# First and last batch of a four-layer graph attention kernel: other order of the first loads, norms by VectorE's statistics, and a last head in two halves

## The chip, the cores and the metric

The kernel runs on one core of one Trainium2 chip. The metric is the device time of one execution in microseconds, lower is better. The engines are named as in the profile: PE is TensorE's matmul (PEld its weight load), DVE is VectorE, ACT is ScalarE, POOL is GpSimd, SP is SyncE. `SPq` and `POOLq` are the queues from which transfers are issued. A line number such as L330 is a line of the kernel before.

## The reference

There are 16 graphs of 1024 nodes with 256 features, and a 0/1 adjacency matrix for each. Four graph attention layers follow one another; each normalizes its input, projects it, weights the neighbours, and adds the result to its input. The first and the last layer, cut to what matters:

```python
# x: (16, 1024, 256), adj: (16, 1024, 1024)
def _layernorm(x, axis=-1, eps=1e-5):
    m = jnp.mean(x, axis=axis, keepdims=True)
    v = jnp.var(x, axis=axis, keepdims=True)
    return (x - m) / jnp.sqrt(v + eps)

# layer 0 (layers 1 and 2 have other activations of the weight and an elu at the end)
h = jnp.maximum(_layernorm(x), 0.0)
Wh = jnp.einsum('bnf,fo->bno', h, W)
f1, f2 = Wh @ a1, Wh @ a2
e = jax.nn.leaky_relu(f1[:, :, None] + f2[:, None, :], negative_slope=0.2)
e = jnp.where(adj == 0, NEG_INF, e)
x = x + jnp.einsum('bij,bjo->bio', jax.nn.softmax(e, axis=-1), Wh)

# layer 3: the same with 4 heads of 64 features (only edges of type 1 occur), and then
out = jax.nn.relu(dst) + h            # dst: attention times values, plus bias
mu, var = out.mean(-1, keepdims=True), out.var(-1, keepdims=True)
out = (out - mu) / jnp.sqrt(var + 1e-6) * ln_gamma + ln_beta
x = x + out                           # heads side by side: 1024 x 256
```

## The kernel before, in words

All of the time below is in `short_path`; a general path stands behind a flag (`bad`) and isn't taken with these inputs. The nodes of a batch lie in eight blocks of 128 partitions; four pairs of blocks share a row of memory, so that a partition of a pair holds two neighbouring nodes (`in_blocks`).

**Two streams.** Even batches form stream 0 and odd batches stream 1. `batch(b)` is a generator that emits instructions and yields estimated times; the loop at the end of `short_path` always advances the stream that is behind, and stream 1 starts 111 (`LAG`) later. So the dependent stretches of one batch lie beside the matmuls of the other. Only at the very start is stream 0 alone, and only at the very end stream 1. The framework then orders each engine's instructions by priority and by a plan of its own; `keep_in_program_order` fixes the order of single instructions.

**Loading.** `load(b)` has POOL issue four transfers that cast a quarter of the adjacency matrix's rows each from int32 to bytes and write them to memory (`narrow`, L125), and then SP issue four transposing transfers (L135), one for each pair of blocks of columns, into `mask`. Each transpose reads all rows, so it waits for all four casts. `fetch_nodes` loads `x_b` with one transfer of 1 MB on SP (L115). The weights come in `prepare`, on SP too: for layers 0 to 2 first W and then the attention vectors `a`, copied to all partitions (L197); L225 multiplies the two and sums, and `extend` (L189) writes the products as extra columns of W.

**Layer 0's norm and projection.** `first(pair)` sums two blocks of x on DVE (L476); `project` scales the sums to `minus_mean` (L282), makes `centered`, max(x - mean, 0), on DVE (L285), and has ACT sum the squares (L292). `inverse_root` makes the reciprocal deviation on POOL with an add (L271) and a power (L272). PE transposes `centered` (L301), ACT copies it out as `hT` (L303), PE multiplies by the extended W (L308), and `evict` (L376 on ACT, L380 on DVE) makes the values V. In later layers the sums come from the end of the layer before.

**Attention.** PE lays the column of scores out as a row on all partitions (L337), DVE makes the weights for each block with one instruction (L330) from row, column and mask, and PE multiplies weights and V (L424).

**The last layer.** For each of four heads PE makes values and totals transposed (L541), ACT copies both out (L618), PE turns them (L625, L633), DVE inverts the totals (L627, L348, L349) and scales (L636) into `y`. Then `center(h)` adds the bias on POOL (L502), adds the projected input and takes the mean off on DVE (L503, L505 to L507), squares on ACT (L509) and sums on DVE (L511), with `inverse_root` on POOL. `rescale`, one head later, multiplies by the reciprocal deviation on DVE (L515), and by gamma and adds x on POOL (L516, L517). All of these work on 128 x 512 elements, a head of all eight blocks. At the end POOL issues two transfers of 512 KB to the output (L650). Squares of the adjacency (L154), which feed the flag, lie in between on ACT.

Of the kernel before, what the change touches and what calls it, by code (L numbers as in the profile page):

```python
# [41 lines left out]
P = 128  # L42
# [19 lines left out]
def short_path(ctx: ExitStack, tc: tile.TileContext, ins: dict, out: bass.AP, bad: bass.AP):  # L62
# [48 lines left out]
    narrows = [dram.tile([N, N // 2], BF, name=f"narrow{n}") for n in range(2)]  # L111

    def fetch_nodes(b: int):
        xs[b] = nodes.tile([P, NI, D], F32, name="x_b")
        fetch = nc.sync.dma_start(xs[b].rearrange("p (c t) f -> p c t f", t=2), in_blocks(x[b]))  # L115
        if b > 0:
            tc.keep_in_program_order(fetch)

    def load(b: int):
# [3 lines left out]
        rows = narrow.bitcast(U8).rearrange("(c t q) j -> c q t j", t=2, q=P)  # L123
        for c in range(NI // 2):
            cast = nc.gpsimd.dma_start(  # L125
                rows[c], adj[b, ts(c, 2 * P), :].rearrange("(q t) j -> q t j", t=2)
            )
            tc.keep_in_program_order(cast)
# [5 lines left out]
        for c in range(NI // 2):  # L134
            turn = nc.sync.dma_start_transpose(  # L135
                mask[:, c].rearrange("p n t -> p (n t)").bitcast(BF), narrow[:, ts(c, P)]
# [36 lines left out]
    def prepare():  # L173
# [21 lines left out]
        def fetch(l: int):  # L195
# [5 lines left out]
            if l < 3:  # L201
                begin(W[l][:, :, :D], ins[f"L{l}_W"].rearrange("(k p) o -> p k o", p=P))
                begin(scratch[l][:, : 2 * D], on_all_partitions(ins[f"L{l}_a"], 2 * D))
                return
# [63 lines left out]
    def inverse_root(squared: bass.AP, n: int, elements: int, eps: float) -> bass.AP:  # L268

        r = small.tile([P, n], F32, name=f"rstd{n}")  # L270
        nc.gpsimd.tensor_scalar_add(r, squared, elements * eps)  # L271
        nc.gpsimd.tensor_tensor(r, r, minus_half.to_broadcast([P, n]), op=ALU.pow)  # L272
        return r
# [4 lines left out]
    def project(b: int, l: int, xb: bass.AP, sums: bass.AP, pair: int, evict):  # L278


        minus_mean = small.tile([P, 2], F32, name="minus_mean")
        nc.vector.tensor_scalar_mul(minus_mean, sums[:, ts(pair, 2)], -1.0 / D)  # L282
        centered = work.tile([P, 2, D], F32, name="centered", bufs=3)
# [12 lines left out]
        rstd = inverse_root(squared, 2, D, LN_EPS)  # L296
# [67 lines left out]
    def batch(b: int):  # L364
# [110 lines left out]
        def first(pair: int):  # L475
            nc.vector.tensor_reduce(sums[:, ts(pair, 2)], xb[:, ts(pair, 2), :], AX.X, ALU.add)  # L476
# [19 lines left out]
        shape = [P, NI, E]  # L496

        def center(h: int):

            yh = y[:, :, h, :]  # L500
# [550 lines left out]
```

## Time and profile before

| what | value |
|---|---|
| median of 3 runs | 2948.88 us (2948.02 to 2951.19) |
| profiled execution, span | 2948.4 us |
| granted TensorE clock, mean | 0.992 |
| PE busy | 2810.6 us, 95% of the span |
| DVE busy | 2124.8 us, 72% |
| ACT busy, POOL busy | 1092.1 us (37%), 980.7 us (33%) |
| first attention weights (L330) start | 26.82 us |
| last attention weights (L330) end | 2908.45 us |
| second output transfer issued (L650) | about 2935.0 us |

PE's share is so high that what counts is where it is not busy. The page's picture in 40 slices shows that only the first slice and the last two fall below 0.9 of PE's time. Two instructions of one group can take different times, and a group's mean hides that, so the timeline is what tells when each step of the first and the last batch ran. The chain of waits names, for each step, what released it; pieces that follow one another on one engine are merged there.

### The profile page before, as it was taken

The page shows a single profiled execution, that of the slowest core. Times are in us where ns is not written, and L with a number is a line of the kernel's source. Part 1 is how long each engine was busy: PE and PEld are TensorE (multiplying, and loading weights), DVE is VectorE, ACT ScalarE, POOL GpSimd, SP SyncE. Part 2 cuts the span into 40 slices and gives each one's busy share as a digit, 9 for nine tenths or more (in the row PEclk, how much of TensorE's full clock was granted, in tenths as well). Part 3 has the DMA queues.
Part 4 walks back from the last instruction along what each step waited for, and adds up shares of the span by engine and source line. Part 5 has one row for each costly group of instructions (what it writes and reads, how often), then busy time and mean ns, then how long its engine had stood idle before and what let it go on. Part 6 is the DMA issues. An engine that isn't in the chain of part 4 may idle for free.

```text
span 2948.4 us, 44754 instructions
## 1 busy us (share of the span) xinstructions
PE 2810.6 (95%) x16790; PEld 1969.3 (67%) x16790; DVE 2124.8 (72%) x4471; ACT 1092.1 (37%) x3025; POOL 980.7 (33%) x1535
## 2 busy tenths in 40 slices
PE   7999999999999999999999999999999999999975
PEld 5775857668576685766758576685766857667551
DVE  5658688585976858678586875859768586785855
ACT  2333434343343433424333343433434334343331
POOL 2123324243233423324233242432334233242333
PEclk9999999999999999999999999999999999999997
DMA  7204022030311303122030220303113031010101
GB/s 123 40 8 65 29 31 56 8 51 29 42 45 19 68 1 51 36 29 58 8 52 29 33 55 8 51 29 45 43 20 67 1 51 36 15 30 8 22 18 27
DMA packets 120495, 106.11 MB, mean 36 GB/s; under 512 B 73680, under 2 KB 91216, under 8 KB 120272
## 3 DMA queue, kind: packets, MB, share of 16 engines
q0 software_dynamic: 40448, 67.12, 15.4%
q1 hardware_dynamic: 79824, 36.05, 5.5%
q8 instruction: 135, 2.21, 0.3%
q14 instruction: 88, 0.72, 0.1%
HBM read 153.49 MB, written 33.55 MB: 63 GB/s over the span
## 4 chain that ended last, share of the span: by engine, by line
PE 60%; DVE 23%; issue 8%; POOL 5%; ACT 3%; DMA 1%; POOLq 0%; SPq 0%; ACTq 0%; DVEq 0%
PE acc L424 36%; DVE weights L330 16%; PE acc L541 11%; PE acc L308 9%; PE misc L301 2%; POOL rstd L272 2%; POOL y L502 2%; ACT square L292 1%; DVE V L380 1%; PE row L337 1%; DVE y L503 1%; DVE var L511 1%; DVE y L507 1%; DVE mean L505 1%; ACT below L356 1%
## 5 line engine op out<-in xcount | busy, mean ns | idle before, releaser
L424 PE MATMUL acc<-V,weights 128*128 128x257 f32 x6144 | 1436.3, 385 | 33.9 <-DVE weights L330 16.7
L424 PEld LDWEIGHTS acc<-V,weights 128*128 128x128 f32 x6144 | 1141.9, 191 | 277.9 <-DVE weights L330 72.0
L541 PE MATMUL acc<-weights,V 128*32 128x512 f32 x6144 | 692.0, 597 | 12.1 <-DVE weights L330 8.1
L330 DVE SCALAR_TENSOR_TENSOR weights<-row,ex,mask 128x1024 f32<-128x1024 f32 x512 | 629.1, 1273 | 97.4 <-PE row L529 66.0
L308 PE MATMUL acc<-W,hT 128*128 128x259 f32 (+1 forms) x2048 | 516.5, 389 | 41.7 <-ACT hT L303 29.2
L330 DVE SCALAR_TENSOR_TENSOR weights<-row,V,mask 128x1024 f32<-128x1024 f32 x384 | 473.8, 1275 | 1.0 <-PE row L337 1.0
L308 PEld LDWEIGHTS acc<-W,hT 128*128 128x128 f32 x2048 | 379.6, 191 | 138.0 <-ACT hT L303 47.1
L541 PEld LDWEIGHTS acc<-weights,V 128*32 128x32 f32 x6144 | 189.6, 110 | 417.6 <-issue 410.7
L356 ACT ACTIVATE below<-acc,inv 128x256 f32<-128x256 f32 x256 | 121.1, 473 | 818.0 <-DVE inv L349 537.3
L272 POOL TENSOR_TENSOR rstd<-rstd,minus_half 128x2 f32<-128x2 f32 (+1 forms) x320 | 302.9, 947 | 20.3
L292 ACT ACTIVATE square<-x_b,minus_mean 128x256 bf16<-128x256 f32 x512 | 259.7, 507 | 111.1 <-DVE minus_mean L282 105.4
L404 POOL TENSOR_TENSOR x_b<-x_b,beta 128x256 f32<-128x256 f32 x128 | 93.4, 730 | 489.8 <-ACT square L292 489.8
L348 DVE TENSOR_SCALAR inv<-acc 128x1 f32<-128x1 f32 x256 | 39.2, 154 | 256.0 <-PE acc L424 254.7
L271 POOL TENSOR_SCALAR rstd<-squared 128x2 f32<-128x2 f32 x256 | 64.6, 253 | 462.8 <-ACT square L292 461.9
L303 ACT ACTIVATE hT<-misc 128x512 f32<-128x512 f32 x256 | 150.1, 592 | 119.7 <-PE misc L301 119.4
L359 DVE SCALAR_TENSOR_TENSOR x_b<-below,x_b 128x256 f32<-128x256 f32 x256 | 133.0, 519 | 85.3 <-ACT below L356 83.2
L618 ACT COPY sums<-acc 128x512 f32<-128x512 f32 x128 | 74.9, 585 | 307.8 <-PE acc L541 300.3
L285 DVE TENSOR_SCALAR centered<-x_b,minus_mean 128x256 f32<-128x256 f32 x512 | 182.6, 385 | 5.3
L376 ACT ACTIVATE V<-acc,rstd 128x3 f32<-128x3 f32 x384 | 98.4, 261 | 232.0 <-PE acc L308 231.3
L380 DVE TENSOR_SCALAR V<-acc,rstd,V 128x256 f32<-128x256 f32 x256 | 131.6, 537 | 62.0 <-ACT V L376 61.1
L301 PE MATMUL misc<-ident,centered 128*128 128x128 f32 x1024 | 157.9, 277 | 15.2 <-DVE centered L285 13.4
L149 POOL DMA_DIRECT2D adj_i<-in_adj_dram x128 | 74.7, 584 | 286.4 <-ACT adj_i L154 254.9
(88 smaller groups left out, 2210.0 us busy)
## 6 DMA issues: line engine op xcount, KB each, us to landing
adj_i<-in_adj_dram POOLq DMA_DIRECT2D x128, 256.0 KB, 3.9
x_b<-in_x_dram SPq DMA_DIRECT2D x16, 1024.0 KB, 6.4
narrow<-in_adj_dram POOLq DMA_DIRECT2D x64, 256.0 KB, 9.5
out_dram<-y POOLq DMA_DIRECT2D x32, 512.0 KB, 7.4
mask<-narrow SPq DMA_TRANSPOSE x64, 3.7
W<-in_L_gnn_W_dram SPq DMA_DIRECT2D x3, 256.0 KB, 5.8
weights<-in_L_gnn_a_dram SPq DMA_DIRECT2D x3, 256.0 KB, 8.1
W<-in_L_gnn_W_dram SPq DMA_DIRECT2D x2, 128.0 KB, 8.3
```

Source lines behind the costliest of these rows:

```text
L272: nc.gpsimd.tensor_tensor(r, r, minus_half.to_broadcast([P, n]), op=ALU.pow)
L285: nc.vector.tensor_scalar(centered[:, n, :], xb[:, 2 * pair + n, :], minus_mean[:, n : n + 1], 0.0, op0=ALU.add, op1=ALU.max,)
L292: nc.scalar.activation(square, xb[:, 2 * pair + n, :], AF.Square, bias=minus_mean[:, n : n + 1], accum_out=squared[:, n : n + 1],)
L301: nc.tensor.transpose(turned[:, k, ts(n, P)], centered[:, n, ts(k, P)], ident)
L303: nc.scalar.mul(hT, turned, ROOT_D)
L308: nc.tensor.matmul(projected, hT[:, k, ts(n, P)], W[l][:, k, :], start=(k == 0), stop=(k == NK - 1),)
L330: nc.vector.scalar_tensor_tensor(w, r, c(j), masks[b][:, j // 2, :, j % 2], op0=op, op1=ALU.mult)
L356: nc.scalar.activation(below, acc[:, :D], AF.Exp, scale=inv)
L359: nc.vector.scalar_tensor_tensor(xi, below, 1.0, xi, op0=ALU.min, op1=ALU.add)
L380: nc.vector.tensor_scalar(V[:, i, :D], projected[:, :D], rstd, V[:, i, D : D + 1], op0=ALU.mult, op1=ALU.mult,)
L424: nc.tensor.matmul(accs[i], weights[j][:, ts(i, P)], V[:, j, : D + 1], start=(j == 0), stop=(j == NI - 1),)
L541: made = nc.tensor.matmul(accT[ts(n, QUAD), :], values, moving, start=first, stop=last)
```

## The change

At the start, the loads of the first batch are meant to arrive in the order in which they are needed, and the norm of layer 0 in batch 0 to pass through fewer engines. `x` comes in four transfers on ACT's queue, one for each pair of blocks. The attention vectors are loaded before W. The casts of the first adjacency matrix are made by halves of its columns (`halves`), each half by two transfers, so that the first two transposes need only the first half. In batch 0 the mean and the variance come from DVE's bn_stats and bn_aggr in place of sums on DVE and squares on ACT.

At the end, in the last batch alone, the bias of the last two heads is added by DVE; the last head is centred and rescaled in two halves of four blocks; the last half's gamma and x steps go to DVE too; and the two outputs are issued by SP and ACT. `inverse_root` gets a factor for the variance and one buffer name for all larger sizes; `inv8` has three buffers for six.

```diff
 def fetch_nodes(b: int):
     xs[b] = nodes.tile([P, NI, D], F32, name="x_b")
+    if b == 0:
+        for c in range(NI // 2):
+            nc.scalar.dma_start(
+                xs[b][:, ts(c, 2), :],
+                x[b, ts(c, 2 * P), :].rearrange("(p t) f -> p t f", t=2),
+            )
+        return
...
+    if b == 0:
+        for h in range(NH):
+            for t in range(2):
+                cast = nc.gpsimd.dma_start(
+                    halves[h].bitcast(U8).rearrange("(c t q) j -> t c q j", t=2, q=P)[t],
+                    adj[b].rearrange("(c q t) j -> t c q j", t=2, q=P)[t, :, :, ts(h, HALF)],
+                )
+                tc.keep_in_program_order(cast)
...
-                mask[:, c].rearrange("p n t -> p (n t)").bitcast(BF), narrow[:, ts(c, P)]
+                mask[:, c].rearrange("p n t -> p (n t)").bitcast(BF),
+                halves[c // NH][:, ts(c % NH, P)] if b == 0 else narrow[:, ts(c, P)],
...
+                begin(scratch[l][:, : 2 * D], on_all_partitions(ins[f"L{l}_a"], 2 * D))
                 begin(W[l][:, :, :D], ins[f"L{l}_W"].rearrange("(k p) o -> p k o", p=P))
-                begin(scratch[l][:, : 2 * D], on_all_partitions(ins[f"L{l}_a"], 2 * D))
...
-        r = small.tile([P, n], F32, name=f"rstd{n}")
-        nc.gpsimd.tensor_scalar_add(r, squared, elements * eps)
+        r = small.tile([P, max(n, NI) if n > 2 else n], F32, name=f"rstd{8 if n > 2 else n}")[:, :n]
+        nc.gpsimd.tensor_scalar(r, squared, times, elements * eps, op0=ALU.mult, op1=ALU.add)
...
+        if sums is None:
+            mv = small.tile([P, 2, nc.vector.BN_AGGR_DIM], F32, name="mv", bufs=2)
+            for n in range(2):
+                stats = small.tile([P, nc.vector.BN_STATS_DIM], F32, name="stats", bufs=1)
+                nc.vector.bn_stats(stats, xb[:, 2 * pair + n, :])
+                nc.vector.bn_aggr(mv[:, n, :], stats)
+                nc.vector.tensor_scalar(
+                    centered[:, n, :], xb[:, 2 * pair + n, :], mv[:, n, 0:1], 0.0,
+                    op0=ALU.subtract, op1=ALU.max,
+                )
+            rstd = inverse_root(mv[:, :, 1], 2, D, LN_EPS, D)
...
+        def center(h: int, blocks=slice(0, NI), engine=nc.gpsimd):
+            yh = y[:, blocks, h, :]
...
-            nc.gpsimd.tensor_add(yh, yh, bias[:, head].unsqueeze(1).to_broadcast(shape))
+            engine.tensor_add(yh, yh, bias[:, head].unsqueeze(1).to_broadcast(shape))
...
+        def rescale(yh: bass.AP, blocks, head, rstd: bass.AP, engine=nc.gpsimd):
             nc.vector.tensor_mul(yh, yh, rstd.unsqueeze(2).to_broadcast(shape))
-            nc.gpsimd.tensor_mul(yh, yh, gamma[:, head].unsqueeze(1).to_broadcast(shape))
-            nc.gpsimd.tensor_add(yh, yh, xb[:, :, head])
+            engine.tensor_mul(yh, yh, gamma[:, head].unsqueeze(1).to_broadcast(shape))
+            engine.tensor_add(yh, yh, xb[:, blocks, head])
...
-            inv = small.tile([P, NH, NG], F32, name="inv8")
+            inv = small.tile([P, NH, NG], F32, name="inv8", bufs=3)
...
-            normed.append(center(h))
+            if b < B - 1:
+                normed.append(center(h))
+            elif h < H - 1:
+                normed.append(center(h, engine=nc.gpsimd if h < H - 2 else nc.vector))
+            else:
+                normed += [center(h, slice(g * NG, g * NG + NG), nc.vector) for g in range(NH)]
...
-        rescale(*normed.pop())
+        while normed:
+            rescale(*normed.pop(0), engine=nc.vector if len(normed) == 0 and b == B - 1 else nc.gpsimd)
         for g in range(NH):
-            nc.gpsimd.dma_start(
+            queue = nc.gpsimd if b < B - 1 else (nc.sync, nc.scalar)[g]
+            queue.dma_start(
```

## The prediction

> **What bounds the kernel now.** I read the page's busy line first, then the stretches, then the chain of waits at both ends with the timeline beside it. The page says that the middle belongs to TensorE:
>
> ```profile
> PE 2810.6 (95%) x16790; PEld 1969.3 (67%) x16790; DVE 2124.8 (72%) x4471; ACT 1092.1 (37%) x3025; POOL 980.7 (33%) x1535
> ```
>
> The span is 2948.4 us, so PE misses 137.8 us in all. The stretches (columns: us, then busy time and count of PE, PEld, DVE, ACT, POOL, clock, DMA share, GB/s) say where much of it lies:
>
> ```profile
> 0.00:20.00 20.00, 7.03 (x25) 5.50 (x26) 8.49 (x36) 7.84 (x22) 7.37 (x18) 1.00 0.80 131
> 150.00:200.00 50.00, 50.00 (x246) 43.63 (x245) 22.45 (x79) 19.89 (x60) 17.20 (x39) 1.00 0.00 1
> ...
> 2920.00:2930.00 10.00, 0.19 (x2) 0.12 (x2) 5.22 (x13) 0.63 (x1) 5.18 (x5) 0.50 0.02 5
> 2930.00:2940.00 10.00, 0.00 (x0) 0.00 (x0) 0.69 (x1) 0.00 (x0) 4.54 (x5) 0.50 0.29 108
> ```
>
> Between the ends PE has no gap to give. The change touches only batch 0's start and batch 15's end, so I price these two chains; a microsecond off either should come off the span. The chain of waits at the start (start us, us, what):
>
> ```profile
> 1.92 8.06 DMA weights<-in_L_gnn_a_dram
> 10.12 0.43 DVE above L225
> 13.16 0.59 DVE sums_of_x L476
> 14.06 1.12 PE misc L301 x4
> 15.18 3.48 PE acc L308 x8
> ...
> 24.01 2.04 PE acc L308 x8
> 26.40 0.43 issue
> 26.82 1.09 DVE weights L330
> 28.02 8.43 DVE weights L330 x7
> ```
>
> The attention vector `a` of layer 0 is the third transfer on SP, lands at 9.98, and L225 (which makes the extra columns of W) holds up VectorE until then, with the first `centered` behind it. The first projection starts at 14.97, the last ends at 26.03, and the first attention weights, which need the row from all eight blocks, start at 26.82. At the other end:
>
> ```profile
> 2912.79 1.25 POOL y L502
> 2914.07 0.70 DVE y L503
> ...
> 2918.28 1.67 POOL rstd L272
> 2919.97 0.70 DVE y L515
> 2920.74 1.27 POOL y L516
> 2922.08 1.26 POOL y L517
> 2923.34 1.23 POOL y L502
> ...
> 2932.60 1.27 POOL y L517
> 2933.87 0.29 issue
> 2934.16 0.82 POOL out_dram L650
> ```
>
> POOL is passed through again and again: the bias of head 2 waits behind the last two steps of head 1, and that of head 3 (2923.34) behind head 2's. The second output is issued at 2935.0; the DMA view has about 4.0 us to landing, so 2939, and 9.4 us of program end follow that no edit touches.
>
> **What the Trainium skill says.** "VectorE: DVE Perf Modes", section on the TRN2 errata, gives (N+151)/0.96 ns for an fp32 tensor_tensor: 691 ns at 512 elements; the trace has 0.69 us at L507 and L515, so 424 ns at 256 is an estimate that I use. "GPSIMD Engine Reference", 4.1 Engine selection, calls POOL about twice as slow as VectorE for two inputs; the trace agrees, 1.26 us at L516 against 0.69. "DMA: Bandwidth & Descriptors", section "Issuing engines are not separate DMA queues": transfers from all issuers share the same 16 engines, so a second queue saves issue time alone. The trace agrees: from 8 to 18.9 us the engines are full with the casts. No page that I found prices bn_stats.
>
> **The change part by part: the start.** `x` goes from one 1 MB transfer to four of 256 KB, on ACT's queue, and `a` goes ahead of W on SP's. Before, x, W and a, 1.5 MB in all, moved from 2.3 us at some 350 GB/s, x landing at 6.46. In halves of that rate, pair 0 of x (with as much of `a` beside it) takes 0.5 MB / 350 GB/s = 1.5 us and lands at about 4.3, `a` with it, W by about 6, the last pair by 7.3. ACT issues four transfers (0.46 us each on SP before); nothing else is in its queue then.
>
> VectorE's statistics: bn_stats over 256 elements is not in the trace. Bound below: a tensor_scalar of 256, 0.35 us (L285). Above: a tensor_reduce of 512, 0.68 (L476). I take the reduce at 256, 0.68 - 256/0.96 ns = 0.41. bn_aggr is a tiny operation, 0.16 like L282. A pair then costs 2 x (0.41 + 0.16 + 0.35) = 1.84, some 2.0 with start gaps, where L476, L282 and 2 x L285 took 0.68 + 0.16 + 0.70 = 1.54: VectorE gains 4 x 0.46 = 1.8 us of work (up to 4 with the upper price). ACT loses eight L292 of 0.50 + 0.19 = 5.5 us. Before, minus_mean and centered could not finish until L225 had its `a`; now pair 0 is centered at 4.3 + 2.0 = 6.3, L225 and its columns (4 x 0.35 + 0.4 = 1.8) come at about 8.2, hT with the 1.28 us table load at about 9.4. So L308 can start at about 9.5 for 14.97. From there to the first weights took 26.82 - 14.97 = 11.85; VectorE's pace is now 2.0 + 2 x 0.55 (L380) = 3.1 us a pair, against 2.0 to 3.0 seen between projections of PE, hardly above it. 9.5 + 11.85 = 21.4, less 26.82: 5.4 us. With the dear bn_stats and L225 late, 2.5.
>
> The masks could take the place of this. Casting batch 0 in column halves moves the same bytes in 2048 pieces for 1024. The half-casts let two of the four transposes start when half 0 is done: the DMA view has 0.07 MB of the cast's output moved by 8 us and then 105 GB/s, so 0.5 MB at 8 + 0.43 / 0.105 = 12.1, say 12.5, where all four waited to 18.9. The DMA work is as much as before and ended about 27, so chunks 2 and 3 land near 25.5 and 27. Weights from 21.4 at 1.2 us each want chunk 2 at 26.2 and chunk 3 at 28.6: just hidden. A 512 B piece could be slower than I reckon; an extra 2 us would still cost only about 1. POOL issues the casts for longer (0.72 us each for 256 pieces, perhaps 1.2 for 512), and the first L271 stands behind that; it is wanted at about 11, so hidden. The new `mv` has two buffers: pair 2's statistics wait for POOL's read of pair 0's, at about 6.6, before VectorE gets there.
>
> The extra multiply in inverse_root rides in the same instruction (L271, 0.25 us), and three `inv8` buffers for six last two heads of each stream: nothing, beside PE's work.
>
> **The end.** Up to L636 of head 2, at 2910.50, nothing changes. Then its bias add runs on VectorE at 2911.2 (0.69) instead of on POOL to 2914.03: the chain L503 to L515 of head 2, which took 2914.07 to 2919.97, can start at about 2912.0, so L515 starts near 2918.0 and ends near 2918.7; the gain is 2.0 us. ACT's copy L618 of head 3 stood behind head 2's square (2917.04) and moves by the same 2 us, so head 3's `y` (L636) is ready between 2917.7 (ahead of L515) and 2919.5 (behind it, as before). I take T = 2918.7.
>
> From T, the two halves. Each VectorE step over 256 elements costs 0.27 us less than at 512. Half 0 by the start gaps of before: bias 0.47, L503 0.47, L505 0.46, L506 0.21, L507 0.51, square 0.46, L511 0.50, L271 0.32, power 1.07 (4 columns: between the 0.71 of 2 and the 1.67 of 8), L515 0.50: T + 5.0. Its gamma and x_b stay on POOL, 0.73 each (L404 at this size). Half 1's VectorE steps fill the gaps, its L511 ends near T + 5.5, its power near T + 6.9 (T + 7.9 if POOL takes half 0's two steps first), L515, gamma and x_b on VectorE 3 x 0.47: T + 8.4 to 9.3. So the last issue is at 2927.1 to 2928.0, for 2935.0. Both outputs come close together, as before (1 MB moved in about 3 us), from two queues: landing 4.0 after issue, as POOL's. The gain is 7 to 7.9; with T's two ends, 6 to 9. I take 7.7. Nothing is queued behind the outputs on SP or ACT but the program's end.
>
> Sum: 5.4 + 7.7 = 13.1, so 2948.9 - 13.1 = 2935.8 us.
>
> **The rivals.** (1) One end pays in part. The start gives 1 to 2, because VectorE, with more work ahead of PE, or the masks set the pace (the DMA engines are full until 18.9, which speaks for it; that L330 came 8 us after the first transposes speaks against), or the end gives only 4, because POOL's power for the two halves queues. 2948.9 - 2 - 6 = 2941. (2) The start's gain is lost in the pipeline: stream 1, which starts near 101 us, waits on batch 1's transposes, issued from 51.8 to 86.9, and the end gives only what one saved POOL round is worth, 4: 2945, no measurable change. Against: no wait in the view to 110 us is for a DMA except at the first 10 us. (3) Slower. The order on each engine is planned ahead, and another start shifts the plan: if all four pairs' statistics (8 us, up to 12 with the upper price) run ahead of L225, the first projection starts no earlier than before; and an interleave of the two streams that is worse by 0.13 us in each of the 64 layer stages costs 8 us, with an end that gains 4: 2953. Against: in the chain the same pieces come back every 178.7 to 178.8 us (399.29, 578.03, 756.78), and their code isn't changed. (4) More: cheap statistics and both ends at their best, 7 + 9: 2933.
>
> **How the numbers follow.** Forecast (2932 to 2940) 0.62, rival 1 0.16, rival 4 and better (below 2932) 0.08, rival 2 0.08, rival 3 0.06. Faster by over 0.2% means below 2943.0: the forecast, rivals 4 and 1: 0.86; same 0.08; slower 0.06. For 8 in 10 the range takes in the forecast, rival 4's core and most of rival 1: 2929 to 2942.5.
>
> **What would show it.** Right: the first L330 at about 21.4; no squares of `x_b` on ACT before it; the first two mask transposes near 12.5; the steady stretches the same, shifted by 5; the last output issued near 2922 in the changed span (2927.6 - 5.4), and PE stopping that much earlier. Wrong: VectorE waiting for mask or for POOL between 8 and 30 us, an L308 that starts after 13, an end longer than 2935.0 - 2908.5 - 5 = 21.5 us from the last weights' end to the last output, or periods other than 178.8.

## The result, and the profile after

The changed kernel takes 2933.01 us in the median of 6 runs (2932.02 to 2934.67), the kernel before 2949.65 us beside it (6 runs, 2948.02 to 2951.19). The ratio is 0.9944, with a 95% interval of 0.9931 to 0.9956: 16.6 us faster. The forecast of 2935.8 us was 2.8 us too high, inside its range. Its single terms are another matter: four of them were off by 3 to 7 us each and cancelled one another. That the sum came out was luck, and most of what follows is about the terms.

The code above L115 of the kernel before has hardly moved, but later lines have. In the changed kernel the weights are L367 (L330 before), the transposes of `centered` L338 (L301), the first projection L345 (L308), the values L413 and L417 (L376, L380), the sums for W L246 (L225), the statistics, their sum and the centering of batch 0 L323 to L325, `inverse_root` L292 and L293 (L271, L272), the last layer's bias L544 (L502), its sum with h L545 (L503), the three steps of `rescale` L560 to L562 (L515 to L517), `y` L681 (L636), the outputs L704 (L650).

The page's first line, of the changed kernel: busy time, share of the span and count of each engine.

```profile
PE 2810.0 (96%) x16790; PEld 1961.9 (67%) x16790; DVE 2147.9 (73%) x4490; ACT 1088.2 (37%) x3010; POOL 981.3 (33%) x1533
```

PE's work is the same to 0.6 us, in a span of 2931.4 us for 2948.4. So all of the gain is time in which PE had stood still. DVE is busy 23 us longer, but most of that is not new work: e3 below adds no DVE instruction and is busy 17.0 us longer than the kernel before (2141.8 us), because the same 512 centering instructions take 416 ns in the mean for 385. More busy time on DVE went with a shorter program there. The first stretch of the changed kernel (us, then busy time and count of PE, PEld, DVE, ACT, POOL, clock, DMA share, GB/s):

```profile
0.00:20.00 20.00, 8.53 (x31) 5.76 (x31) 10.77 (x46) 4.09 (x8) 8.69 (x17) 1.00 1.03 130
```

In the first 20 us ACT's work fell from 7.84 to 4.09 us (the squares are gone) and DVE's rose from 8.49 to 10.77, while PE gained only 1.5 us.

Three marks cut the two profiled spans into four parts: the start of the first attention weights, the end of the last, and the start of the last output's issue.

| part of the span | before | after | gain | forecast |
|---|---|---|---|---|
| to the first weights | 26.82 | 25.40 | 1.4 | 5.4 |
| first weights to the end of the last | 2881.63 | 2877.23 | 4.4 | 0 |
| last weights to the start of the last output's issue | 26.6 | 22.2 | 4.4 | 7.7 |
| from there to the end of the span | 13.4 | 6.6 | 6.8 | 0 |
| sum | 2948.4 | 2931.4 | 17.0 | 13.1 |

**The start.** The chain of waits of the changed kernel (start us, us, what):

```profile
1.33 6.30 DMA W<-in_L_gnn_W_dram
...
25.40 6.18 DVE weights L367 x6
```

W now ends the wait that `a` ended before, at 7.63 us for 9.98. From the first projection at 12.7 to the first weights the trace shows 12.7 us. In it, the statistics of the later pairs stand in DVE's queue behind the values L417 of the first pair, which wait for PE and ACT; pair 2's begin at 16.78 (the lines stand at e5 below). The masks are no wait: the six weights from 25.40 follow one another without a gap.

**The end.** The timeline of the changed kernel, DVE, POOL and the two output queues (start us, us, engine, line, operation, out and in, count):

```profile
2906.13 1.65 DVE L545 SCALAR_TENSOR_TENSOR y<-y,h 128x512 f32<-128x512 f32 x1
...
2913.83 0.69 DVE L681 TENSOR_TENSOR y<-misc,inv 128x512 f32<-128x512 f32 x1
...
2914.55 2.08 DVE L544 TENSOR_TENSOR y<-y,bias 128x256 f32<-128x256 f32 x2
2915.03 1.32 POOL L562 TENSOR_TENSOR y<-y,x_b 128x512 f32<-128x512 f32 x1
...
2924.83 0.41 ACTq L704 DMA_DIRECT2D out_dram<-y  x1
```

Where a DVE instruction with two inputs in SBUF, the memory that the engines share, meets one of POOL, it takes much longer: L545 takes 1.65 us beside L562 of head 1, for 0.70 at the same place before, and the two halves of the last bias 2.08 us beside L562 of head 2. Alone, a half takes 0.42. L681 isn't slowed: at 2913.83 it runs beside L561 of POOL (2913.69 to 2914.95) and takes 0.69 us. One of its two inputs, `misc`, lies in PSUM, where PE puts its results.

The last part of the table is not in any view of waits. The records of POOL's sequencer show it (ns, shortest, median and longest, then the first and the last start in us), first in the kernel before, then in the changed one:

```profile
L1014 POOLq INC_SWDGE_SEM  x1: 1732/1732/1732, 2939.4 to 2939.4; - x1
L1047 POOLq DRAIN  x3: 50/107/6361, 2941.2 to 2948.1; - x3
```

```profile
L1068 POOLq INC_SWDGE_SEM  x1: 936/936/936, 2924.7 to 2924.7; - x1
L1101 POOLq DRAIN  x3: 46/107/3091, 2925.7 to 2931.1; - x3
```

A semaphore increment and a drain come last on POOL, 1.73 + 6.36 us in the kernel before and 0.94 + 3.09 us now. In the kernel before they begin at 2939.4, 4.4 us after POOL's second output is issued, which is about when it lands. In the changed kernel POOL issues no last output, so they begin at 2924.7 and lie beside the transfers.

### The profile page after: what moved, and what is told of

Its sections match the earlier page's. It is cut to its first block, busy times and chain, and to the rows that moved or that the text cites. A ratio compares the mean times of both kernels' runs of the same rounds, so it can differ in the third digit from the quotient of the medians.

```text
span 2931.4 us, 44756 instructions
## 1 busy us (share of the span) xinstructions
PE 2810.0 (96%) x16790; PEld 1961.9 (67%) x16790; DVE 2147.9 (73%) x4490; ACT 1088.2 (37%) x3010; POOL 981.3 (33%) x1533
## 3 DMA queue, kind: packets, MB, share of 16 engines
q0 software_dynamic: 47328, 66.10, 15.4%
## 4 chain that ended last, share of the span: by engine, by line
PE 59%; DVE 26%; issue 8%; POOL 3%; ACT 3%; DMA 0%; POOLq 0%; ACTq 0%; SPq 0%; DVEq 0%
PE acc L461 36%; DVE weights L367 16%; PE acc L586 10%; PE acc L345 9%; PE misc L338 2%; DVE centered L302 2%; POOL rstd L293 2%; DVE V L417 1%; PE row L374 1%; POOL y L544 1%; DVE y L545 1%; DVE var L555 1%; ACT square L309 1%; DVE y L551 1%; DVE mean L549 1%
## 5 line engine op out<-in xcount | busy, mean ns | idle before, releaser
L367 DVE SCALAR_TENSOR_TENSOR weights<-row,ex,mask 128x1024 f32<-128x1024 f32 x512 | 629.0, 1272 | 97.3 <-PE row L574 65.8
L345 PE MATMUL acc<-W,hT 128*128 128x259 f32 (+1 forms) x2048 | 516.1, 389 | 38.1 <-ACT hT L340 26.9
L367 DVE SCALAR_TENSOR_TENSOR weights<-row,V,mask 128x1024 f32<-128x1024 f32 x384 | 473.7, 1273 | 0.8 <-PE row L374 0.8
L345 PEld LDWEIGHTS acc<-W,hT 128*128 128x128 f32 x2048 | 378.7, 190 | 135.1 <-ACT hT L340 44.4
L293 POOL TENSOR_TENSOR rstd<-rstd,minus_half 128x2 f32<-128x2 f32 (+1 forms) x321 | 292.8, 912 | 20.3
L292 POOL TENSOR_SCALAR rstd<-squared 128x2 f32<-128x2 f32 x252 | 80.0, 317 | 464.0 <-ACT square L309 451.0
L302 DVE TENSOR_SCALAR centered<-x_b,minus_mean 128x256 f32<-128x256 f32 x504 | 195.7, 416 | 5.1
L413 ACT ACTIVATE V<-acc,rstd 128x3 f32<-128x3 f32 x384 | 98.4, 261 | 231.1 <-PE acc L345 230.6
L417 DVE TENSOR_SCALAR V<-acc,rstd,V 128x256 f32<-128x256 f32 x256 | 131.4, 537 | 59.8 <-ACT V L413 58.9
L338 PE MATMUL misc<-ident,centered 128*128 128x128 f32 x1024 | 158.7, 277 | 13.7 <-DVE centered L325 11.5
```

Of the source, the lines that this page charges most:

```text
L302: nc.vector.tensor_scalar(centered[:, n, :], xb[:, 2 * pair + n, :], minus_mean[:, n : n + 1], 0.0, op0=ALU.add, op1=ALU.max,)
L338: nc.tensor.transpose(turned[:, k, ts(n, P)], centered[:, n, ts(k, P)], ident)
L345: nc.tensor.matmul(projected, hT[:, k, ts(n, P)], W[l][:, k, :], start=(k == 0), stop=(k == NK - 1),)
L367: nc.vector.scalar_tensor_tensor(w, r, c(j), masks[b][:, j // 2, :, j % 2], op0=op, op1=ALU.mult)
L417: nc.vector.tensor_scalar(V[:, i, :D], projected[:, :D], rstd, V[:, i, D : D + 1], op0=ALU.mult, op1=ALU.mult,)
```

## The experiments

"First weights" is the start of the first L330 or its counterpart, "tail" the time from the end of the last weights to the end of the span, both of the profiled execution; the last column is POOL's increment and drain.

| kernel | median us | ratio, 95% interval | first weights | tail | POOL's end |
|---|---|---|---|---|---|
| before | 2949.7 to 2951.5 | | 26.8 | 39.9 | 1.7 + 6.4 |
| after | 2933.01 | 0.9944 (0.9931 to 0.9956) | 25.4 | 28.8 | 0.9 + 3.1 |
| e1 | 2937.11 | 0.9957 (0.9944 to 0.9971) | 25.7 | 32.6 | 1.0 + 3.3 |
| e2 | 2944.52 | 0.9982 (0.9974 to 0.9989) | 25.9 | 34.6 | 1.7 + 6.2 |
| e3 | 2945.96 | 0.9988 (0.9981 to 0.9994) | 25.6 | 39.7 | 1.7 + 6.4 |
| e4 | 2944.31 | 0.9982 (0.9974 to 0.9989) | 25.8 | 36.0 | 1.0 + 3.3 |
| e5 | 2934.17 | 0.9944 (0.9930 to 0.9957) | 23.7 | 30.8 | 1.7 + 6.2 |
| e6 | 2934.33 | 0.9945 (0.9932 to 0.9959) | 23.8 | 31.3 | 1.8 + 6.6 |
| e7 | 2937.05 | 0.9952 (0.9938 to 0.9965) | 26.2 | 28.9 | 0.9 + 3.1 |
| e8 | 2933.56 | 0.9942 (0.9929 to 0.9956) | 25.8 | 28.6 | 0.9 + 3.1 |
| e9 | 2944.59 | 0.9977 (0.9967 to 0.9986) | 24.6 | 29.1 | 0.9 + 3.0 |
| e10 | 2940.09 | 0.9962 (0.9949 to 0.9976) | 29.5 | 30.8 | 1.7 + 6.2 |
| e11 | 2932.41 | 0.9934 (0.9920 to 0.9947) | 24.0 | 29.1 | 1.7 + 6.2 |
| e12 | 2933.08 | 0.9940 (0.9926 to 0.9953) | 27.1 | 29.3 | 1.7 + 6.2 |

The medians come from several groups of runs, and the kernel before itself moves by 1.8 us between them; across groups the ratios are the better guide. One caution for the "first weights": each is from one profiled execution. The kernels that share the old start (before, e2, e3) spread from 25.6 to 26.8 us, mean 26.1; those that share the new one (after, e1, e4, e8) from 25.4 to 25.8, mean 25.7. By these means the start as changed is worth 0.4 us, less than the spread; a difference below 1 us between two single profiles says nothing there.

### The outputs' queue

**e1, the changed kernel with the outputs issued by POOL**

```diff
-            queue = nc.gpsimd if b < B - 1 else (nc.sync, nc.scalar)[g]
+            queue = nc.gpsimd
```

> The changed kernel with the last two outputs issued by POOL again. Theory A (POOL's drain at the program's end is what the outputs' queue was worth): from the start of the last issue to the end of the span 13 us where the changed kernel has 6.6 and the kernel before 13.4, POOL's last drain about 6.4 us for 3.1; time 2933.0 + 6.8 = about 2940. Rival B (only the issue itself differs, 0.8 us a piece for 0.4): drain and end gap as in the changed kernel, time about 2934.

It takes 2937.11 us, 4.1 more than the changed kernel, and its tail is 3.8 us longer. The time from the last issue's start to the span's end is 10.1 us for 6.6. Theory A has the direction, and rival B is out; but the drain stayed short (3.3 us, not 6.4), so the queue is not all that had changed at the end. e4 shows what else.

**e2, the kernel before with batch 15's outputs issued by SP and ACT**

```diff
-            nc.gpsimd.dma_start(
+            queue = nc.gpsimd if b < B - 1 else (nc.sync, nc.scalar)[g]
+            queue.dma_start(
```

> The kernel before with only the last two outputs issued by SP and ACT. Theory A: the gap from the last issue to the end falls from 13.4 to about 6.6 us, POOL's drain hides beside the transfers, time 2949.6 - 7 = about 2942.5. Rival B: time 2948.5 to 2949, and the gap stays above 11.

This one edit alone makes the old kernel 5.3 us faster, and the tail goes from 39.9 to 34.6. The transfers take 4.2 and 4.4 us to land, no less than POOL's 4.0. POOL's increment and drain, 7.9 us here, no longer begin when the second output has landed but at 2934.1, when POOL's last sum is done, and 9.2 us remain from the last issue to the end for 13.4. The other 1.1 us of the tail come from the issues themselves, which no longer follow one another on POOL. Theory A's 6.6 us were not reached: the long drain outlasts the transfers. So the 9.4 us of program end that the prediction called untouchable were in good part touched by the choice of queue.

### The middle

**e3, the kernel before with the two-operation form in `inverse_root`**

```diff
-        nc.gpsimd.tensor_scalar_add(r, squared, elements * eps)
+        nc.gpsimd.tensor_scalar(r, squared, 1.0, elements * eps, op0=ALU.mult, op1=ALU.add)
```

> The kernel before with only inverse_root's first instruction changed to a multiply by 1 and an add. Theory C (the two-operation form is behind the 4.4 us by which the steady part of the changed kernel runs ahead, though every engine's order of instructions there is the same): the last weights end 4.4 us earlier than in the kernel before, 2904.0 for 2908.5, period 178.5 for 178.8, time about 2945. Rival D (the 4.4 us come from the shifted start, which lets the two streams and the transfers fall differently): last weights at 2908.5 as before, time 2949.6.

A multiply by one, in one line, makes the old kernel faster: ratio 0.9988 (0.9981 to 0.9994). The chain of waits shows it as a shorter period. Lines of the same piece in neighbouring batches (start us, us, what), first the kernel before, then e3:

```profile
1830.37 6.95 issue
...
2009.10 6.96 issue
```

```profile
1826.88 6.96 issue
...
2005.40 6.96 issue
```

Subtract the two: 178.73 us before, 178.52 in e3; the changed kernel has 178.51 (1825.37 and 2003.88). Over some 15 periods 0.22 us is 3.3 us, and Theory C holds. In e4, which has the whole new start but the old one-operation form elsewhere, the period is 178.74. So the form of this one instruction carries the shorter period, and the order of the two streams has no part in it: in the steady batches each engine's list of instructions is the same before and after. Where PE gains is on the profile's page. The line of the projections L308, of the kernel before and of e3 (after the bar: busy us and mean ns, then PE's idle time before them and what ended most of it):

```profile
L308 PE MATMUL acc<-W,hT 128*128 128x259 f32 (+1 forms) x2048 | 516.5, 389 | 41.7 <-ACT hT L303 29.2
L308 PE MATMUL acc<-W,hT 128*128 128x259 f32 (+1 forms) x2048 | 515.7, 388 | 38.3 <-ACT hT L303 27.0
```

PE's waits before its projections fall by 3.4 us, about the whole gain; the changed kernel has 38.1, e4 with the old form 41.6. How POOL's instruction reaches these waits is less clear. The 8-column instruction is shorter (198 ns in the mean for 246), but the 2-column one is longer in the mean (319 for 253) though shorter in the median (193 for 222), and the power behind it fell from 766 to 731. A few instructions now start at other moments and meet others of DVE. Which meeting it is was not isolated.

A rest stays open. Between weights 352 and 464, in batches 6 to 8, all kernels with the new start gain some 0.8 us more in one place, e4 too, and e3 doesn't.

### The start

**e4, the changed kernel with the old end and the one-operation form outside batch 0**

```diff
-        nc.gpsimd.tensor_scalar(r, squared, times, elements * eps, op0=ALU.mult, op1=ALU.add)
+        if times == 1.0:
+            nc.gpsimd.tensor_scalar_add(r, squared, elements * eps)
+        else:
+            nc.gpsimd.tensor_scalar(r, squared, times, elements * eps, op0=ALU.mult, op1=ALU.add)
...
+            normed.append(center(h))
...
+            rescale(*normed.pop(0))
...
+            queue = nc.gpsimd
```

> The changed kernel with the end of before (bias on POOL, whole last head, outputs on POOL) and with the one-operation add in inverse_root outside batch 0: only the new start is left. Theory C: the first weights start at 25.4 as in the changed kernel, 1.4 us ahead of before, and the last weights end at about 2907.0, still 1.4 us ahead; time about 2948.2. Rival D: the lead grows to 5.8 us, last weights at 2902.6, time about 2943.8.

It gains 5.5 us over the kernel before, but hardly any of it at the start. The first weights come at 25.8 us. The tail went from 39.9 to 36.0, with an end that is word for word the old one: POOL's increment and drain fell to 1.0 + 3.3 us. The change at the start shortened the end of the program. The time alone would have pointed to rival D (2943.8), and wrongly: the last weights end at 2906.75, as Theory C said, not at 2902.6.

**e5, the changed kernel with batch 0's casts by row blocks, as before**

```diff
-        if b == 0:
-            for h in range(NH):
-                ...
-        else:
+        if True:
...
-                halves[c // NH][:, ts(c % NH, P)] if b == 0 else narrow[:, ts(c, P)],
+                narrow[:, ts(c, P)],
```

> The changed kernel with the first adjacency matrix cast by four quarters of rows, as before. Theory E (the casts by halves did nothing for the start, and shortened only what POOL does at the program's end): first weights at 25.4 within the 1.3 us by which they vary among runs of one start, first transpose at 18.9; POOL's last INC_SWDGE_SEM and DRAIN 1.7 and 6.3 us as in the kernel before, for 0.9 and 3.1, which then sets the end: about 2 us more from the last issue to the end, time about 2935. Rival F (the early half of the mask carries the start): first weights 2 us later or with a wait before the third pair's, POOL's drain 3.1, time about 2935 with the loss at the start.

The same time within the interval, and two gains have changed places: first weights at 23.7 us for 25.4, which neither theory expected, and POOL's end back at 1.7 + 6.2 us, which now sets the end, as Theory E said. So the order of the loads and DVE's statistics are worth about 2.4 us (the old starts' mean of 26.1 less 23.7; the kernels e9 and e11, with the same start as e5, have 24.6 and 24.0), the half casts as written go with a loss of most of that, and pay for it with a shorter drain.

The loss is not a wait for the casts. It goes with another order of DVE's instructions. DVE's timelines, first of the changed kernel, then of e5, whose L314 and L408 are L323 and L417 there:

```profile
15.05 0.54 DVE L417 TENSOR_SCALAR V<-acc,rstd,V 128x256 f32<-128x256 f32 x1 [1.38 <-ACT V L413]
...
16.78 0.41 DVE L323 BATCH_NORM_STATS2 stats<-x_b 128x6 f32<-128x256 f32 x1
```

```profile
13.63 0.42 DVE L314 BATCH_NORM_STATS2 stats<-x_b 128x6 f32<-128x256 f32 x1
...
15.10 0.54 DVE L408 TENSOR_SCALAR V<-acc,rstd,V 128x256 f32<-128x256 f32 x1 [0.44 <-ACT V L404]
```

Until 13.6 us the two run alike. Then the changed kernel's DVE stands idle for 1.38 us, because both values of the first pair come ahead of pair 2's statistics; in e5 the first block of pair 2 fills this gap. The other runs agree: e1, e4 and e8 have the changed kernel's order and first weights at 25.7 to 25.8 us, e6, e9 and e11 have e5's order and 23.8 to 24.6. Why the framework's plan chose the worse order with these casts is open, and no run changed the order alone.

**e6, the half casts with the 128 rows as the slowest dimension**

```diff
-     halves[h].bitcast(U8).rearrange("(c t q) j -> t c q j", t=2, q=P)[t],
-     adj[b].rearrange("(c q t) j -> t c q j", t=2, q=P)[t, :, :, ts(h, HALF)],
+     halves[h].bitcast(U8).rearrange("(c t q) j -> t q c j", t=2, q=P)[t],
+     adj[b].rearrange("(c q t) j -> t q c j", t=2, q=P)[t, :, :, ts(h, HALF)],
```

> The changed kernel with the half casts' rows walked with the 128-row dimension outside and the dimension of 4 inside, same bytes. Theory G (by the Trainium skill, DMA: Bandwidth & Descriptors, the number of engines of one transfer follows its slowest dimension: 4 there, 16 here): the four casts no longer land together near 19; half 0 lands near 12 and the first two transposes start near 12.5, the other two near 19.5. The first weights still start near 25, since the row and not the mask sets them: time within 2 of the changed kernel. Rival H (the pattern has nothing to do with it; the small pieces are slow): the first transpose stays near 19.5.

SP's timeline, first of the changed kernel, then of e6 (start us, us from the first to the last of the four):

```profile
19.50 5.69 SPq L155 DMA_TRANSPOSE mask<-narrow_half  x4
```

```profile
14.45 7.74 SPq L155 DMA_TRANSPOSE mask<-narrow_half  x4
```

Only the order of two dimensions differs, and the first transposes start 5 us earlier. The Trainium skill, "DMA: Bandwidth & Descriptors", section "Why a DMA increments its semaphore by 16 and not by 1", says that the slowest dimension decides over how many engines a transfer is spread. In the casts as written it is 4, here 128, and the traces agree: with 4 the first half was ready at 19.5 us and the second, as the third transpose shows, at 22.6, with 128 at 14.4 and 19.7. And still the first weights come at 23.8 us, as with the old casts. So the early masks, which the half casts were made for, hide nothing: DVE and the first projections set the start. The drain is long again (1.8 + 6.6 us), so casting by halves is not what shortens it.

**e7, the moments of batch 0 in one buffer for all pairs**

```diff
-            mv = small.tile([P, 2, nc.vector.BN_AGGR_DIM], F32, name="mv", bufs=2)
+            mv = moments[0][:, ts(pair, 2), :]
...
+        if b == 0:
+            moments.append(small.tile([P, NI, nc.vector.BN_AGGR_DIM], F32, name="mv", bufs=1))
```

> The changed kernel with the moments of all eight blocks in one buffer, where two buffers serve four pairs. Theory I (the two buffers made the plan put the statistics of pairs 2 and 3 behind the values of pair 0 on DVE, and these waited for PE until 14.8): all eight statistics end by about 17, first weights at about 24.2 for 25.4 and the time 1 us less, about 2932. Rival J (PE's own work or the landing of x sets the first weights): first weights at 25.4 or later, time 2933 or more.

DVE's timeline then has the last of the statistics done at 16.8 us, ahead of all values. The first weights come at 26.2, no earlier, since the first values now wait at 18.35: a third order of the same instructions, with no gain either. The later stages of batch 0 lose some 1.6 us on top, but e2, whose start is the old one, shows the same loss at the same place in its profile, so it can't be put down to this buffer. The median is 4 us above the changed kernel's, with runs from 2934.3 to 2937.85, and the ratios' intervals overlap: no gain is shown, and how much is lost is open.

**e10, old casts, x's four pieces issued by SP ahead of `a` and W**

```diff
-                nc.scalar.dma_start(
+                nc.sync.dma_start(
```

> The changed kernel with batch 0's casts by row blocks as in the kernel before, and x's four pieces issued by SP, ahead of a and W, and not by ACT. Theory C (two issuing engines at once moved the first bytes slower than one: 0.34 MB by 4 us against 0.48 MB): pair 0 of x lands at about 4.3 us (6.2 with ACT as issuer), the first values start near 11, the first weights at about 22 (23.7), and the time is some 1.5 us below the 2934 us of the same kernel with ACT's queue. Theory D (the DMA engines' start-up sets it, whoever issues, or the later a and W give it back): pair 0 at 5 to 6 us, first weights 23.5 to 25, 2933.5 to 2935 us.

DVE's timeline of e10, whose L314 and L237 are L323 and L246 (the idle time before, and what ended it, in brackets):

```profile
3.74 0.43 DVE L314 BATCH_NORM_STATS2 stats<-x_b 128x6 f32<-128x256 f32 x1 [2.69 <-DMA x_b<-in_x_dram]
...
15.54 0.42 DVE L237 CUSTOM_DVE_ANT_0 above<-W,weights 128x256 f32<-128x256 f32 x1 [7.58 <-DMA W<-in_L_gnn_W_dram]
```

Half of each theory holds. Pair 0 of x is there at 3.74 us, against 6.00 in e5, about when the prediction had it. Whether that is because one queue issues or because `a` no longer moves beside x, this run can't tell; e12 can. But `a` and W then stand behind all of x. In the records of the DMA packets the casts begin at 4.5 us, and beside them W takes until 15.5. First weights at 29.5, and 2940.09 us, 6 us worse than e5.

**e12, old casts, gamma and x of the last head on DVE, only x's first piece issued by SP**

```diff
-                nc.scalar.dma_start(
+                (nc.sync if c == 0 else nc.scalar).dma_start(
```

> The changed kernel with batch 0's casts by row blocks as before, both halves of the last head's gamma and x on DVE, and x's first piece issued by SP ahead of a and W; x's other three pieces stay on ACT. Theory G (what needs pair 0 waits for its bytes, which two queues at once bring at half pace): pair 0 lands at 4.0 to 5.0 us (6.0 when ACT issues it behind nothing, 3.7 when SP issues it alone), DVE centers both of its halves before W lands near 8, so that the first values start about 1 us earlier and the first weights at about 22.8 us (23.95 without this): 2931.3 us. Theory H (ACT's three other pieces take the same DMA engines at the same time, or a and W come later by what x gains): pair 0 at 5.5 us or later, or W at 8.5 or later, first weights at 23.5 to 25 us, 2932.0 to 2933.5 us.

DVE's timeline of e12:

```profile
4.64 0.43 DVE L314 BATCH_NORM_STATS2 stats<-x_b 128x6 f32<-128x256 f32 x1 [3.59 <-DMA x_b<-in_x_dram]
```

Against e11, the kernel without this line, 2933.08 us for 2932.41, no difference by the intervals, as Theory H said. In the profiled execution pair 0 was there at 4.64 us for 6.17, and W at 11.27 for 7.92: what x gains, W loses. This execution was the slowest of the five (2935.56; the others 2932.8 to 2933.1), so its first weights at 27.1 are not typical.

It also speaks against Theory C of e10 and Theory G: SP and ACT issue at once here, and still 0.55 MB had moved by 4 us, as with one issuer (0.48 in the kernel before, 0.57 in e10), for 0.34 in the changed kernel and 0.39 in e5. So two queues at once are not what is slow. In the two slow kernels `a` goes first on SP's queue, beside x, and in the three others x does. That `a`, one row copied to all partitions, holds up the others would fit, but no run loads it alone.

### The end

**e8, the changed kernel with head 2's gamma and x on DVE**

```diff
-                rescale(*normed.pop())
+                rescale(*normed.pop(), engine=nc.vector if b == B - 1 and h == H - 1 else nc.gpsimd)
```

> The changed kernel with gamma and x of the last batch's head 2 on DVE too. Theory K (DVE's steps on two tensors stand still while POOL works on two tensors, which stretched the two bias steps of head 3 from 0.84 to 2.08 us): the two bias steps take 0.42 each; DVE gets 1.4 us more work, so the end moves by only about +0.2, time 2933. Rival L (the long bias steps are due to their shape): they stay near 1 us each, and the end comes 1.4 us later, 2934.4.

DVE's timeline of e8, at the place of the 2.08 us:

```profile
2916.17 0.75 DVE L544 TENSOR_TENSOR y<-y,bias 128x256 f32<-128x256 f32 x2
```

With POOL idle the same two instructions take 0.75 us in all. Theory K holds. That is the lock on the port that DVE and POOL share, which the Trainium skill describes in "SBUF — State Buffer", section "SBUF: two separate sides"; the traces agree, with 2.08 beside POOL and 0.75 alone. The time doesn't move (2933.56), because DVE now has the two steps of 0.68 us in its own queue ahead of the bias. What the port took, the additional work takes.

**e11, old casts, gamma and x of both halves of the last head on DVE**

```diff
-            rescale(*normed.pop(0), engine=nc.vector if len(normed) == 0 and b == B - 1 else nc.gpsimd)
+            rescale(*normed.pop(0), engine=nc.vector if b == B - 1 else nc.gpsimd)
```

> The changed kernel with batch 0's casts by row blocks as in the kernel before, and in the last head both halves' multiply by gamma and sum with x on DVE (half 0's was POOL's). Theory E (POOL's share of half 0 stretches DVE's steps of half 1 over the port, and its packets are no part of the end): last output issue about 0.5 to 1 us earlier, counted from the last weights; but the end is set by POOL's increment and drain (1.7 + 6.2 us with these casts), which start when POOL's last instruction, half 1's power, is done, some 1.5 us earlier than before: tail about 29.5 us for 30.8, time about 2933. Theory F (DVE is the bound of the end and now carries two more instructions of 0.42 us each): last issue 0 to 0.8 us later, tail 30.8 or more, 2934 to 2935 us.

As Theory E said, POOL's work ends with half 1's power, so its long drain starts earlier; it ends at 2930.2 us, 0.8 us before the end of the span, and still sets it. The tail falls from 30.8 to 29.1, the last issue comes 0.5 us sooner after the last weights. At 2932.41 us (2931.96 to 2932.72) it is the best median of the study. It is 0.6 us below the changed kernel, and the two ratios' intervals overlap, so it isn't shown to be faster; but its casts are those of the other batches.

**e9, the half casts moved from batch 0 to batch 8**

```diff
-        if b == 0:
+        if b == 8:
...
-                halves[c // NH][:, ts(c % NH, P)] if b == 0 else narrow[:, ts(c, P)],
+                halves[c // NH][:, ts(c % NH, P)] if b == 8 else narrow[:, ts(c, P)],
```

> The changed kernel, with batch 0's casts by row blocks as in the kernel before and the four half casts, as written, moved to batch 8, in the middle of the program. Question: why POOL's last two instructions (the semaphore increment and the drain) took 0.94 + 3.09 us with the half casts in batch 0 and 1.7 + 6.2 us without them. Theory A (the software queue's state at the end follows from the number and order of its descriptors over the whole program): 0.9 + 3.1 us again, tail from the last weights to the end about 28.8 us; first weights at about 23.7 us as with the old casts; so 2931.0 to 2932.5 us. Theory B (it comes from the casts standing first in the queue): 1.7 + 6.2 us, tail about 30.8 us, and 2934 us as with the old casts. Both: the transposes of batch 8 are hidden, no wait on a mask there.

On the question asked, the answer is plain: 0.9 + 3.0 us at the end, with the casts in the middle of the program. So it doesn't matter that they stand first: one matrix cast in this form, in batch 0 or in batch 8, goes with the short drain. On the time both expectations failed, by 11 to 14 us. They named the transposes as hidden, which they are (SP issues them at 1159.5, about when e5 does), and forgot the plan. POOL's timeline in e9:

```profile
1155.80 0.19 POOL L292 TENSOR_SCALAR rstd<-squared 128x2 f32<-128x2 f32 x1
1167.08 1.64 POOL L544 TENSOR_TENSOR y<-y,bias 128x512 f32<-128x512 f32 x1 [11.09 <-DVE y L681]
1168.68 0.70 POOL L293 TENSOR_TENSOR rstd<-rstd,minus_half 128x2 f32<-128x2 f32 x1
```

The casts take POOL longer to issue (4.42 us for 2.8), the framework's plan is another one around them, and it puts the bias of a head between the two instructions of one `inverse_root`. The bias waits 11 us for `y`; the power waits behind it, and with it the other stream. The kernel is some 3 us ahead of the kernel before when batch 8's casts are issued, and 8 us behind it after this wait.

## Why the prediction was right or wrong

**The total** was in the range and close to the point, by luck: the start and the computing at the end gave 7.3 us less than forecast, and two terms priced at nothing gave 11.2. Of the signs of being wrong that the prediction named, two came true, 22.2 us from the last weights to the last output for at most 21.5, and a period of 178.51 us for 178.8; the sign of being right that mattered most, first weights at 21.4, did not.

**The start: 5.4 us forecast, 1.4 in the profile.** The steps in their order:

- The loads. "In halves of that rate": pair 0 of x at about 4.3 and W at about 6. Measured 6.25 and 7.63. This is where it first failed: the rate of the kernel before, which had 0.48 MB moved by 4 us, was carried over to the new order of the loads, which had 0.34. e10 and e12 reach 0.57 and 0.55 with x first on SP's queue, from one issuer and from two. That `a` ahead of W and beside x is the cause is likely, and not shown.
- bn_stats 0.41, bn_aggr 0.16, centering 0.35: measured 0.43, 0.18, 0.35. The squares are gone from ACT. Right.
- First projection at 9.5: 12.7. W is 1.6 us late; then the second half of pair 0 stands behind L246 in DVE's queue (centered at 10.26), and when `hT` is copied out at 11.65, the transposes of pair 1, which are ready at 12.24, still stand ahead of L345 in PE's queue.
- 11.85 us from there to the first weights: 12.7. DVE's pace was "hardly above" PE's; in fact pairs 2 and 3 queue behind the values, in an order that e5 shows to go with some 1.6 us.
- Half 0's masks at 12.5: 19.5, because the half casts as written use fewer engines (e6 has 14.45). It didn't matter for the weights (e6).
- The casts' issue, "perhaps 1.2" us each: 1.10, and hidden, as said. `mv`'s two buffers: no loss shown (e7).

Undoing the casts (e5) leaves 23.7, so without them the start would have given 2 to 3 us, near the lower case (2.5) in the prediction's own working.

**The middle: 0 forecast, 4.4 in the profile.** "The extra multiply in inverse_root rides in the same instruction (L271, 0.25 us) [...] nothing, beside PE's work." The step took an instruction off the critical path for one without effect. e3 shows 0.21 us per batch from it, some 3.3 of the 4.4. That PE is busy 50.00 us of 50 in the stretch shown didn't mean that the steady batches have no waits: over the program PE stood idle for 41.7 us before its projections alone, and this is where e3 gains.

**The end: 7.7 us forecast to the last issue, 4.4 in the profile.** The structure held, and the term was mis-sized: bias of head 2 on DVE at 2.7 us after the last weights as said, two halves, two queues. The sizes failed in one way. Every DVE step was priced alone. L545 of head 2 took 1.65 for 0.70, so that L560 of head 2 came 0.7 us late and `y` of head 3 behind it, at 11.9 us after the last weights for 10.25. From there to the last issue it took 10.3 us for 8.4 to 9.3: the two biases 2.08 for 0.94, half 1's L560 0.94 and L561 0.83 for 0.47 each, all beside POOL. e1 against e4 gives 36.0 less 32.6, 3.5 us of tail for the whole rearrangement of the last head.

**The program's end: "9.4 us of program end follow that no edit touches".** This was the largest error, 6.8 us. The prediction counted a second queue as saved issue time alone, and left out what POOL still has to do after its transfers. Two edits touch it. The outputs on SP and ACT let POOL's increment and drain run beside the transfers: 3.8 us (e1 against the changed kernel), 5.3 alone (e2). The half casts as written shorten them from about 8 to 4 us: 3.9 where they stand behind the last issue (e4), 2.0 where they don't (e5 against the changed kernel). The chain of waits ended with the issue of the output, so the time after it looked like a constant. What in the casts shortens the drain is open; e9 shows only that it works from batch 0 and from batch 8, and e6 that halves with the other order of dimensions don't do it.

**The rivals.** The first (one end pays in part) describes the start well. Without the two unpriced terms the time would have been about 2943.8 (2949.65 less 1.4 and 4.4), past its 2941 and close to the second rival's 2945. The third, that the plan shifts, didn't come true here, but e9 shows that it was a fair fear: some 11 us from one pair of instructions in another order. In a small way it did come true, in DVE's order at the start (e5).

## What to carry to other kernels

Ask what runs after the last instruction that the chain of waits names: on POOL, which issued software transfers, it costs 4 to 8 us here. With the last outputs on other queues it runs beside them: the short one is then hidden (6.6 us from the last issue to the end), the long one only in part (9.2 in e2, 8.6 in e5, 7.4 in e11, where POOL is done before the last issue). Price a DVE step with two inputs in SBUF for both cases, alone and beside POOL, when moving work off POOL only in part. When an edit changes instructions in a program that is ordered by a plan, compare the order on each engine before reading its time, even where the edit is only to a transfer (e5, e9). And take a sum that came out for no proof of its terms before each has been measured.

## What was not expected of the hardware

- POOL's increment and drain at the end take 0.9 to 1.0 + 3.0 to 3.3 us in the kernels that cast one matrix by halves with 4 as the slowest dimension, and 1.7 to 1.8 + 6.2 to 6.6 us in all others. With the short one the software queue had 47328 to 47616 packets, with the long one 40160 to 41184: more packets, shorter drain. Most of the added ones are small: the pages count 6192 more under 512 bytes in the changed kernel than in the one before. What links them is not known.
- A tensor_scalar of two operations on POOL with 8 columns takes 198 ns (e3) where the add alone takes 246 (the kernel before), in the mean.
- With `a` first on SP's queue and x on ACT's, the first 256 KB of x were there at 6.0 to 6.25 us (e5 and the changed kernel). With x first on SP's queue they were there at 3.74 (e10, one issuer) and 4.64 (e12, two issuers).
